# Recurrent network on one core: four PSUM banks each for gates and values in the attention, the spreading of 1/std in the layer norm, and another recurrent layer

## The chip, the cores and the metric

The kernel runs on one core of a Trainium2 chip. The metric is the time of one execution on the device in microseconds. All data is in float32. The engines are TensorE (PE, with its weight loads shown apart as PEld), VectorE (DVE), ScalarE (ACT), GpSimd (POOL) and SyncE (SP), which here only issues DMAs. Each engine works through its own instructions in order; semaphores hold it where it needs another's result.

## What is computed

The input x is an image of 256 by 256 positions with 32 channels. Four layers are added onto it, each on a group-normalised copy.

```python
x = x + L0(_gn(x))      # layer norm, value and gate products, sigmoid, output product
x = x + L1(_gn(x))      # 3x3 mean, two Sobel filters, magnitude
x = x + L2(_gn(x))      # the same once more
x = x + L3(_gn(x))      # recurrent: 256 sequences of 256 steps, two layers of 128 units

# L0: the softmax is summed over the axis that is contracted with it, so it adds up to 1:
o = sigmoid(mn @ Wg) * (mn @ Wv);   return o @ Wo + bo        # mn = layer norm over channels
# L3, one step; z = x_t @ W_lat + b_lat, then for both layers j:
zz = concat([z, h[j]]) @ W_cell[j] + b_cell[j]
zz = group_norm(zz, 4 groups) * gn_gamma[j] + gn_beta[j]
i, f, o, g = split(zz, 4)
c = sigmoid(f) * c + sigmoid(i) * tanh(g);   h = sigmoid(o) * tanh(c);   z = z + h
# x_hat = x_t + z @ W_out + b_out
```

In the inputs the recurrent norm's weights gn_gamma are 1 and gn_beta are 0.

## The kernel before

The image lies in SBUF as 64 blocks of four rows by 32 channels on the 128 partitions, with the 256 sequences (positions along the other axis) on the free axis: `xa`, and a second copy `xb`. Work on it goes two blocks (512 columns) at a time, 32 such pairs, counted by k.

**Layer norm (L193 to L240).** Per pair, a product with `cen` subtracts the mean over channels (`pc`), ACT squares it, DVE writes it to `xb`, and four products with one column per block give the variances (`pvar`). After eight pairs the 1/std of the batch is computed, transposed and kept in `rstdt`. The framework's scheduler sets the order here.

**Attention (L244 to L314).** `normed(k)` multiplies 1/std back onto the channels: four products with the constant `spread` (`pb`, L256), a product on DVE (L265), and weight and bias on POOL (L267). `gate(u)`, one half (128 of 256 channels) of a pair, does four gate products and four value products, each on 32 rows for one row of the block, all in a pool of six PSUM banks (`pgv`, L277); ACT takes the sigmoid (L283), DVE the product (L285). `project(u)` collects the output in `po` (L293), two units later. The order is written out by hand.

**Recurrence (L557 to L743).** The 256 sequences are two halves h of 128, and there are two layers l, so that one time step has four units (l, h), each with its own PSUM bank `zz` of 128 sequences by 512 gate values. A unit's chain is, by the names of the plan: x, the product with the input (33 rows, one of them the bias); i, the product with layer 0's new state (layer 1 only); m, the product with its own last state; sq, the squares on ACT; rd, their sums on DVE; pw, the power -1/2 on POOL; nz, the scaling on DVE; sg and tg, sigmoid and tanh on ACT; ig, fc and c, the new cell (DVE, POOL, DVE); th, its tanh on ACT; h, on DVE; T, the transpose on TensorE; e, its copy to SBUF on ACT, for the next m. Means are zero by construction, since weights and bias have been centred per gate.

The dictionary `PLAN` gives each operation a time within a step of `PERIOD`; all operations of all steps are sorted by it, and written out in that order. So the numbers set the order in every queue, and nothing else: on the chip each engine runs on as soon as its inputs are there.

In the version before, inputs and `fx` lie twice, at partitions 0 and 64; "x" of a unit issues two 33-row products, one for each layer, in different row groups. The output sums (`emit`) are done once in four steps, as products of 32 columns wide, eight of them. `recurrent_weights` tests on DVE whether the norm's weights are 1 and 0 (`off`, `least`, `flag`), and a branch takes one of two arms; with these inputs it is the one where nz is one multiplication.

## Time and profile before

| what | value |
|---|---|
| median of 3 runs | 3559.14 us (3511.32 to 3562.1) |
| the profiled execution's own time | 3559.14 us |
| its span (first to last instruction) | 3557.3 us |
| PE busy | 91% |
| DVE busy | 77% |
| ACT busy | 57% |
| POOL busy | 49% |

By stretch, from the trace's table of windows: the input and its transposes until 52 us; layer norm 52 to 163.5; attention and its group norm 163.5 to 487; the two Sobel layers 487 to 919; weights of the recurrence 919 to 955.5; the recurrence 955.5 to 3551; the last output until the end.

How to read it: a share is busy time over the span. A group's row names line, engine, operation, what it writes and reads with its shape, and how often; then the busy time in us, the mean duration of one in ns, and after a second bar the idle time ahead of it and what ended that. In timelines the first two numbers are start and length in us. A float32 product shows as two records (x2), each with its own weight load on PEld. The granted clock is TensorE's, as a share of the full one.

### The profile page before, as it was taken

The numbers are of one execution on the slowest core, as the hardware profiler recorded it, in microseconds if no ns is written. First come the engines' busy times: TensorE is split into PE (matmuls) and PEld (weight loads), VectorE is DVE, ScalarE is ACT, GpSimd is POOL, SyncE is SP. The second block draws the span as 40 slices with busy tenths as digits, with TensorE's granted clock in tenths as the row PEclk, the third lists the DMA queues.
The fourth block names the chain that finished last, engine by engine and source line by source line (L and its number), as shares of the span: only waits on it lengthen the run. The fifth ranks groups of instructions, "written<-read, shape, count | busy, mean of one in ns | idle before, by whom it ended". The sixth has DMA issues, their size and how long they took to land.

```text
span 3557.3 us, 40880 instructions
## 1 busy us (share of the span) xinstructions
PE 3245.7 (91%) x11221; PEld 1349.6 (38%) x11221; DVE 2728.8 (77%) x6064; ACT 2037.8 (57%) x5784; POOL 1747.8 (49%) x2358
## 2 busy tenths in 40 slices
PE   6999988798799999999999999999999999999998
PEld 4643356576333333333333333333333333333332
DVE  3267786686588888888888888888888888888886
ACT  3244443333366666666666666666666666666665
POOL 0000034454355555555555555555555555555554
PEclk7599999999799999999999999999999999999998
DMA  3000000000100000000000000000000000000000
GB/s 108 0 1 1 1 1 1 1 1 1 30 7 7 13 13 7 15 7 13 7 13 7 13 13 7 13 10 13 8 12 7 12 8 13 13 9 14 1 7 7
DMA packets 29944, 38.52 MB, mean 11 GB/s; under 512 B 6244, under 2 KB 22917, under 8 KB 29704
## 3 DMA queue, kind: packets, MB, share of 16 engines
q1 hardware_dynamic: 27392, 33.57, 3.3%
q10 hardware_dynamic: 2312, 2.25, 0.2%
q8 instruction: 90, 1.47, 0.2%
q14 instruction: 150, 1.23, 0.1%
HBM read 10.63 MB, written 8.39 MB: 5 GB/s over the span
## 4 chain that ended last, share of the span: by engine, by line
PE 76%; DVE 8%; ACT 7%; issue 3%; POOL 3%; DMA 0%; ACTq 0%; POOLq 0%; DVEq 0%
PE zz L628 26%; PE zz L612 15%; PE zz L623 15%; PE pgv L277 6%; ACT hT L691 4%; PE pt L687 3%; POOL ss L387 2%; PE px L701 2%; PE po L293 2%; PE pc L217 2%; DVE pp L348 1%; PE pvar L225 1%; DVE zn L648 1%; DVE dh L354 1%; PE pb L256 1%
## 5 line engine op out<-in xcount | busy, mean ns | idle before, releaser
L628 PE MATMUL zz<-wc,hT 128*128 128x512 f32 x2040 | 1083.3, 633 | 161.6 <-ACT hT L691 152.8
L644 POOL TENSOR_TENSOR rs<-ve,mhalf 128x4 f32<-128x4 f32 x1024 | 1053.5, 1029 | 208.4 <-DVE ve L641 208.0
L673 POOL TENSOR_TENSOR fc<-ga,c 128x128 f32<-128x128 f32 x1020 | 466.0, 457 | 881.1 <-ACT ga L664 870.9
L648 DVE TENSOR_TENSOR zn<-zz,rs 128x512 f32<-128x512 f32 x1024 | 700.8, 684 | 128.3 <-POOL rs L644 128.3
L641 DVE TENSOR_REDUCE ve<-sq 128x4 f32<-128x516 f32 x1024 | 699.8, 683 | 63.2 <-ACT sq L636 47.9
L636 ACT ACTIVATE sq<-zz 128x512 f32<-128x512 f32 x1024 | 605.9, 592 | 114.8 <-PE zz L628 109.6
L691 ACT COPY hT<-pt 128x128 f32<-128x128 f32 x1024 | 248.2, 268 | 655.1 <-PE pt L687 650.8
L612 PE MATMUL zz<-fx,xt 33*128 33x512 f32 x2048 | 585.7, 644 | 11.3 <-DVE zn L648 7.6
L623 PE MATMUL zz<-wc,hT 128*128 128x512 f32 x1024 | 578.1, 646 | 0.0
L664 ACT ACTIVATE ga<-zn 128x384 f32<-128x384 f32 x1024 | 535.8, 523 | 61.2 <-DVE zn L648 61.2
L628 PEld LDWEIGHTS zz<-wc,hT 128*128 128x128 f32 x2040 | 325.1, 189 | 528.9 <-ACT hT L691 408.8
L669 DVE TENSOR_TENSOR c<-ga 128x128 f32<-128x128 f32 x1024 | 331.9, 324 | 106.0 <-ACT ga L666 105.5
L684 DVE TENSOR_TENSOR h<-ga,th 128x128 f32<-128x128 f32 x1024 | 331.3, 324 | 70.7 <-ACT th L681 57.5
L677 DVE TENSOR_TENSOR c<-c,fc 128x128 f32<-128x128 f32 x1020 | 294.5, 289 | 82.2 <-DVE c L669 2.3
L681 ACT ACTIVATE th<-c 128x128 f32<-128x128 f32 x1024 | 313.5, 306 | 63.7 <-DVE c L677 63.6
L666 ACT ACTIVATE ga<-zn 128x128 f32<-128x128 f32 x1024 | 314.1, 307 | 0.0
L612 PEld LDWEIGHTS zz<-fx,xt 33*128 33x128 f32 x2048 | 156.2, 185 | 405.0 <-DVE c L677 334.5
L623 PEld LDWEIGHTS zz<-wc,hT 128*128 128x128 f32 x1024 | 152.6, 188 | 389.7 <-issue 388.9
L687 PEld LDWEIGHTS pt<-ident,h 128*128 128x128 f32 x1024 | 144.1, 141 | 350.9 <-DVE h L684 228.2
L687 PE MATMUL pt<-ident,h 128*128 128x128 f32 x1024 | 247.1, 281 | 13.3 <-DVE h L684 5.9
L267 POOL TENSOR_SCALAR mn<-mn,gamma,beta 128x512 f32<-128x512 f32 x32 | 24.7, 771 | 444.5 <-DVE mn L265 444.5
L283 ACT ACTIVATE sg<-pgv 128x512 f32<-128x512 f32 x256 | 139.1, 597 | 171.2 <-PE pgv L277 164.3
(130 smaller groups left out, 2720.6 us busy)
## 6 DMA issues: line engine op xcount, KB each, us to landing
xt<-xa SPq DMA_DIRECT2D x256, 64.0 KB, 2.0
nat<-in_x_dram SPq DMA_DIRECT2D x16, 512.0 KB, 6.4
out_dram<-st SPq DMA_DIRECT2D x32, 256.0 KB, 2.3
wc<-in_L_conv_W_cell_dram ACTq DMA_DIRECT2D x2, 512.0 KB, 4.1
kt<-in_consts_dram ACTq DMA_DIRECT2D x1, 832.0 KB
wv<-in_L_conv_Wv_dram ACTq DMA_DIRECT2D x4, 32.0 KB, 4.4
wg<-in_L_conv_Wg_dram ACTq DMA_DIRECT2D x4, 32.0 KB, 4.3
gamma<-in_L_conv_ln_gamma_dram ACTq DMA_DIRECT2D x4, 0.1 KB, 6.7
```

What stands on the lines that cost most here:

```text
L612: nc.tensor.matmul(zz, lhsT=x, rhs=fx[rows, l, :], start=True, stop=l == 0 and t == 0)
L623: nc.tensor.matmul(get("zz"), lhsT=v["hT", 0, t][:, seqs], rhs=wc[:, l, 0, :], start=False, stop=t == 0)
L628: nc.tensor.matmul(get("zz"), lhsT=v["hT", l, t - 1][:, seqs], rhs=wc[:, l, 1, :], start=False, stop=True,)
L636: nc.scalar.activation(sqs[l, h][:, :, 0:H], four(get("zz")), AF.Square, scale=float(H**-0.5))
L641: nc.vector.tensor_reduce(ve, sqs[l, h], AX.X, ALU.add)
L644: nc.gpsimd.tensor_tensor(rs, get("ve"), mhalf, ALU.pow)
L648: nc.vector.tensor_mul(four(zn), four(get("zz")), get("rs").unsqueeze(2).to_broadcast([P, 4, H]))
L664: nc.scalar.activation(ga[:, 0 : 3 * H], get("zn")[:, 0 : 3 * H], AF.Sigmoid)
L669: nc.vector.tensor_mul(c, gates(get("ga"), 0), gates(get("ga"), 3))
L673: nc.gpsimd.tensor_mul(fc, gates(get("ga"), 1), get("c"))
L687: nc.tensor.transpose(pt[:, 0:P], get("h"), ident)
L691: nc.scalar.copy(v["hT", l, t][:, seqs], get("pt")[:, 0:P])
```

## The change

**Norm and attention.** `rstdt` becomes a small tile per batch. The `pb` products, their product on DVE and the weights on POOL move from `normed` into the norm's loop, right behind the batch's transpose, in place on `xb`; `pc` and `pb` have two banks each. In the attention, gates and values get pools of four banks each, and the output `pg` of `project` takes one of the gates' banks. The order is gate, value, next gate, value, project for the pair before.

```diff
-        name="ps_ln", bufs=3, space=PSUM
+        name="ps_ln", bufs=2, space=PSUM
...
-            nc.scalar.copy(rstdt[:, bat, :], ptr)
+            rstdt = lnp.tile([P, P], F32, name="rstdt", bufs=2)
+            nc.scalar.copy(rstdt, ptr)
+            for i in range(KB):
+                k = bat * KB + i
+                pb = ps_ln.tile([P, 2, 2, P], F32, name="pb", bufs=2)
+                for b in range(2):
+                    for h in range(2):
+                        r = (i * 2 + b) * 2 + h
+                        nc.tensor.matmul(
+                            pb[:, b, h, :],
+                            lhsT=spread[:, r * J : (r + 1) * J, :].rearrange("p j c -> p (j c)"),
+                            rhs=rstdt,
...
+                nc.vector.tensor_mul(xc, xc, pb.rearrange("p b h s -> p (b h s)"))
+                nc.gpsimd.tensor_scalar(xc, xc, gamma4, beta4, ALU.mult, ALU.add)
...
-        name="ps_at", bufs=6, space=PSUM
-    ) as ps_at, tc.tile_pool(name="ps_o", bufs=1, space=PSUM) as ps_o:
+        name="ps_g", bufs=4, space=PSUM
+    ) as ps_g, tc.tile_pool(name="ps_v", bufs=4, space=PSUM) as ps_v:
...
+            gate(0)
+            for k in range(NST):
+                value(2 * k)
+                gate(2 * k + 1)
+                value(2 * k + 1)
+                if k >= 1:
+                    project(k - 1)
+                if k + 1 < NST:
+                    gate(2 * k + 2)
+            project(NST - 1)
```

**Recurrence.** The test, the branch and the second copy of inputs go. x is one product of all 128 rows, of which 95 are zero. The squares are four activations, one per gate, that sum as they go; `ve` on POOL adds the epsilon. nz is four operations that also multiply by gamma, and bz adds beta. One sigmoid covers all four gates; the tanh of g is 2 sigmoid(2g) - 1, with the factor 2 in gamma and beta, and ig is (s - 0.5) times the input gate, with th scaled by 2. For the output, hs adds the two layers' states on POOL, and one product per step with `woutz` (zero outside 32 columns) sums it. The plan's PERIOD is 10.34 instead of 8.78, with other times.

```diff
-        rows = slice(l * X1, l * X1 + KX)
-        x = xts[blk // XT % NX][rows, blk % XT, j, h * P : (h + 1) * P]
-        nc.tensor.matmul(zz, lhsT=x, rhs=fx[rows, l, :], start=True, stop=l == 0 and t == 0)
+            x = xts[blk // XT % NX][:, blk % XT, j, seqs]
+            nc.tensor.matmul(zz, lhsT=x, rhs=fx[:, l, :], start=True, stop=l == 0 and t == 0)
...
-            nc.scalar.activation(
-                sqs[l, h][:, :, 0:H], four(get("zz")), AF.Square, scale=float(H**-0.5)
-            )
-        elif name == "rd":
-            nc.vector.tensor_reduce(ve, sqs[l, h], AX.X, ALU.add)
+            for g in range(4):
+                nc.scalar.activation(
+                    sq, gates(get("zz"), g), AF.Square, accum_out=ss[:, g : g + 1]
+                )
+        elif name == "ve":
+            nc.gpsimd.tensor_scalar(ve, get("ss"), 1.0 / H, CELL_EPS, ALU.mult, ALU.add)
...
-                nc.vector.tensor_mul(
-                    four(zn), four(get("zz")), get("rs").unsqueeze(2).to_broadcast([P, 4, H])
-                )
+            for g in range(4):
+                nc.vector.scalar_tensor_tensor(
+                    gates(zn, g),
+                    gates(get("zz"), g),
+                    get("rs")[:, g : g + 1],
+                    gates(gam[:, l, :], g),
+                    ALU.mult,
+                    ALU.mult,
+                )
+        elif name == "bz":
+            nc.vector.tensor_add(get("zn"), get("zn"), bet[:, l, :])
...
-            nc.scalar.activation(ga[:, 0 : 3 * H], get("zn")[:, 0 : 3 * H], AF.Sigmoid)
-        elif name == "tg":
-            nc.scalar.activation(gates(get("ga"), 3), gates(get("zn"), 3), AF.Tanh)
+            nc.scalar.activation(ga, get("zn"), AF.Sigmoid)
...
+        elif name == "hs":
+            nc.gpsimd.tensor_add(v["hs", t][:, seqs], v["hT", 0, t][:, seqs], v["hT", 1, t][:, seqs])
...
+        nc.tensor.matmul(px, lhsT=woutz[:, j, :], rhs=v["hs", t], start=False, stop=j == J - 1)
...
-PERIOD = 8.78
+PERIOD = 10.34
 PLAN = {
+    (0, 0): dict(x=-2.2, m=0, sq=1.5, ve=2.8, pw=3.08, nz=4.16, bz=5.2, ga=5.95, fc=7.22, ig=7.6),
+    (0, 1): dict(x=2.96, m=5.17, sq=6.67, ve=7.97, pw=8.25, nz=9.33, bz=10.37, ga=11.12, fc=12.39),
+    (1, 0): dict(x=9.18, i=11.45, m=12.45, sq=13.72, ve=15.02, pw=15.3, nz=16.38, bz=17.34),
+    (1, 1): dict(x=14.35, i=16.62, m=17.62, sq=18.89, ve=20.19, pw=20.47, nz=21.55, bz=22.51),
 }
+PLAN[0, 0].update(c=7.9, th=8.35, h=8.71, T=9.07, e=9.71)
+PLAN[0, 1].update(ig=12.78, c=13.07, th=13.52, h=13.88, T=14.24, e=14.88)
+PLAN[1, 0].update(ga=18.17, ig=18.85, fc=19.57, c=20.51, th=20.87, h=21.32, T=21.68, e=21.98, hs=22.31)
+PLAN[1, 1].update(ga=23.34, ig=24.02, fc=24.74, c=25.68, th=26.04, h=26.49, T=26.85, e=27.15, hs=27.48)
```

## The prediction

> **What bounds the kernel now.** I read the table of busy time by stretch first, then the chain of waits and the timeline inside one time step, then the groups. The stretches (columns: stretch, length, then busy time and instructions of PE, PEld, DVE, ACT, POOL, then the granted clock, DMA share, GB/s):
>
> ```profile
> 52.00:163.50 111.50, 110.07 (x324) 76.54 (x324) 28.01 (x37) 23.93 (x39) 0.00 (x0) 0.50 0.00 0
> 163.50:487.00 323.50, 318.90 (x1793) 127.02 (x1793) 224.26 (x352) 141.96 (x259) 24.83 (x34) 0.97 0.00 1
> 955.50:3551.00 2595.50, 2416.90 (x7412) 832.88 (x7412) 2126.41 (x5180) 1686.42 (x5183) 1500.27 (x2047) 0.99 0.04 10
> ```
>
> These are the layer norm, the gated attention and the recurrence. The recurrence is 73% of the span: 2595.5/256 = 10.14 us a step, so 0.1 us a step is worth 25.6 us, more than most edits elsewhere. The chain of waits inside two steps says what holds it:
>
> ```profile
> by line: PE zz L628 34.6%; PE zz L612 25.2%; PE zz L623 23.1%; ACT hT L691 5.2%; PE pt L687 4.5%; DVE zn L648 2.8%; PE px L697 2.1%; DVE st L718 2.0%; issue 1.6%; PE pf L717 1.1%; DVE h L684 1.0%
> ```
>
> TensorE's three gate products are 83% of the chain. The timeline tells what one product costs (start, length, engine):
>
> ```profile
> 2002.40 1.98 PE L628 MATMUL zz<-wc,hT 128*128 128x512 f32 x4 [0.25 <-ACT hT L691]
> ...
> 2002.93 0.19 PEld L628 LDWEIGHTS zz<-wc,hT 128*128 128x128 f32 x1 [0.24 <-ACT ga L664]
> ...
> 2003.36 0.19 PEld L628 LDWEIGHTS zz<-wc,hT 128*128 128x128 f32 x1 [0.24 <-issue]
> ...
> 2004.31 0.30 PEld L612 LDWEIGHTS zz<-fx,xt 33*128 33x128 f32 x4 [0.76 <-DVE c L677]
> 2004.31 1.13 PE L612 MATMUL zz<-fx,xt 33*128 33x512 f32 x4
> ...
> 2005.37 0.30 PEld L623 LDWEIGHTS zz<-wc,hT 128*128 128x128 f32 x2 [0.76 <-issue]
> 2005.37 1.12 PE L623 MATMUL zz<-wc,hT 128*128 128x512 f32 x2
> ...
> 2008.82 1.13 PE L628 MATMUL zz<-wc,hT 128*128 128x512 f32 x2 [0.35 <-ACT hT L691]
> ```
>
> One product alone takes 1.13 us (2008.82), two of them together 1.98: the second adds 0.85, because its weights were loaded at 2002.93 while the first still ran. Around the 33-row x products nothing is loaded ahead: the loads at 2004.31 and 2005.37 start when the product before has ended, and each product fills 1.06 us. A step now has four m, two i and two pairs of x (a pair runs side by side in 1.06).
>
> **The recurrence, engine by engine.** TensorE: the x products become four full-height ones. Ten full-height products at 0.85 are 8.5 us, four transposes at 0.11 (chain) 0.45, and the output sums, now 1.25 products of 256 columns a step at 0.43 (L697 in the chain) plus transposes, 0.6. That is 9.6 us a step: more work than before, but it fits into 10.14, and the order puts an x product between each transpose and the m that needs it, where PE now stands still (0.35 us at 2008.82). So what is late next are the other engines.
>
> The Trainium skill speaks against my 0.85: "TensorE: Matmul & The Clock Gate", The mechanism, has weight loads overlap running matmuls only where the row groups differ. By that rule every product would cost 1.06 and TensorE alone 11.7 us a step. The row at 2002.93, both full height, shows the overlap, and the x rows show none where the row groups change; I go by the rows.
>
> The other engines per unit (four units a step), with the rows they come from:
>
> ```profile
> L644 POOL TENSOR_TENSOR rs<-ve,mhalf 128x4 f32<-128x4 f32 x1024 | 1053.5, 1029 | 208.4 <-DVE ve L641 208.0
> L648 DVE TENSOR_TENSOR zn<-zz,rs 128x512 f32<-128x512 f32 x1024 | 700.8, 684 | 128.3 <-POOL rs L644 128.3
> L636 ACT ACTIVATE sq<-zz 128x512 f32<-128x512 f32 x1024 | 605.9, 592 | 114.8 <-PE zz L628 109.6
> ```
>
> - sq: one 592 ns activation becomes four 128x128 ones that also sum. No row has a summing activation. Short activations start 0.20 us apart here (2009.77, 2009.97, 2010.17) and last 0.31 (L681); the ends are 0.20 and 0.31 and more. I take 0.29, near the upper end, since the sum must also be written; the new plan leaves 1.16 for four. First start to last end: 3x0.29+0.31 = 1.18.
> - the 683 ns reduction on DVE (L641) goes; ve, 128x4 on POOL, comes: 0.32 (L341; 0.22 to 0.60), with 0.05 of handing over 0.37.
> - pw stays at 1.03.
> - nz: one 684 ns product becomes four scalar_tensor_tensor of 128x128, 0.34 each (L535, a single one), started 0.26 apart if they overlap by the 0.08 that plain products show (0.28 long, 0.20 apart); ends 0.20 and 0.34. Then bz, an addition of 128x512, 0.68, that needs them and 0.1 for the dependence (L669 at 2005.17 for 0.28, L677 at 2005.56): 3x0.26+0.34+0.1 = 1.22 to its start.
> - sg and tg become one sigmoid of 512, 0.63 long (L664's 0.52 plus 0.11 for 128 more); ig becomes 0.34; hs adds 0.46 on POOL (L673's shape).
>
> All queues are in order, and the order is written out by hand. Walking round it, the longest loop in half a step goes from one layer's squares to the other half's: squares 1.18, ve 0.37, pw 1.03, hand-over 0.03, nz 1.22, bz until the next start 0.60, ig until c may start 0.44, c 0.32 with hand-over, th until the next sq may start 0.20. Sum **5.39 us**. A second loop (nz, the other half's c, bz, ga 0.53, e 0.20, sq) has 5.31. TensorE needs 4.8, and the pure dependence of layer 0 on itself 8.4 a step, so neither is the bound. On top: the output's fin (0.47 on ACT) and st (0.42 on DVE) every fourth step and px ahead of an m, 0.1 a half step; and one conflict:
>
> ```profile
> 492.27 0.71 DVE L348 TENSOR_TENSOR pp<-u,xn 128x508 f32<-128x508 f32 x1
> ...
> 494.27 1.42 POOL L352 TENSOR_TENSOR sh<-v 128x512 f32<-128x512 f32 x1
> 494.71 1.52 DVE L348 TENSOR_TENSOR pp<-u,xn 128x508 f32<-128x508 f32 x1
> ```
>
> The same DVE addition took 0.71 alone and 1.52 beside a POOL addition. The new bz is such an addition, and by the walk fc (0.46 on POOL) falls on its start: between 0 and 0.3 a half step; I take 0.07, the loops having some play. Half a step 5.56, a step **11.1 us**: (11.1-10.14)x256 = **+246 us**. The ends: squares 0.20, nz 0.20 apart and no conflict give 9.95 a step (-49 us); squares 0.35, nz 0.34 apart and the full conflict 12.3 (+553 us).
>
> **Norm and attention.** These lines are one unit of attention (9.77 us for two units and one pb):
>
> ```profile
> 196.12 1.14 PE L277 MATMUL pgv<-mn,wg 32*128 32x512 f32 x8
> 197.08 2.45 PE L277 MATMUL pgv<-mn,wv 32*128 32x512 f32 x8
> 198.20 2.48 DVE L285 TENSOR_TENSOR o<-pgv,sg 128x512 f32<-128x512 f32 x4 [2.22 <-PE pgv L277]
> 199.47 1.06 PE L293 MATMUL po<-o,wo 128*32 128x512 f32 x8
> ```
>
> The value products take 2.45 instead of 1.14 since with six banks they wait for sigmoids to free them. With four banks for each, PE needs 4x0.96 + 1.92 = 5.8 a pair and DVE 2x2.4 + 1.4 (L302, L303) = 6.2. The project's 1.9, the next gate's 0.96 and a first value's 1.1 stand in PE's order ahead of the next o: 0.1 to 0.2 (last value's end) + 4.1 against 3.8 of DVE work leaves some 0.5 idle: 6.8. Saved: (9.77-6.8)x32 = 95 us, and of the 11 us that the stretch holds beyond 32x9.77, for filling, I leave 6: 100. pb moves into the norm, which has PE full at clock 0.50: its 8 records took 2.0 to 2.1 us there (164 to 176 us) against 1.16 later: 32x2.0 = +64 if the clock stays. pb also makes that stretch denser, so some of it may run at the full clock: I take +40, so **-60**; ends -14 (+64, and 7.5 a pair) and -118 (the norm no longer than now with pb in it, at the full clock, and 6.3 a pair). DVE's product (0.69) and POOL's 0.77 lie beside PE there.
>
> The page's States table (same title, What's actually happening) has the clock rise after 3.4 us of sustained work; by that the norm, 99% busy, should be at full clock already and pb cost 37 us. The row says 0.50 for 111 us.
>
> **The start of the recurrence.** Now 11 us of memsets (L572) run after the weights are done at 943.7, behind the branch; the first reduction waits for them until 955.6. Without the branch they go ahead, beside the weights; the 3.6 us of flag tests on DVE go too. **-10** (0 to -13). x loads are halved to four per block; SP has room either way.
>
> Sum, against the profiled execution's 3559.1 us, which is also the median of the three: 3559+246-60-10 = **3735 us**.
>
> **Rivals.** A, *TensorE is relieved and nothing replaces it*: squares start 0.20 apart, scalar_tensor_tensor 0.20, step 9.95: 3559-49-70 = 3440, faster. For: the short activations at 2009.77 to 2010.17 start 0.20 apart, and an x product stands where PE now waits. Against: the sum's extra write, and DVE then holds 9 to 10 us. It decides from a step under 10.13, where the other parts' 70 us are the whole change. B, *the play swallows most of it*, step 10.13 to 10.69 (the plan writes 10.34): about 3556, no change. C, *conflict and serial small instructions*, step 11.9: 3559+451-70 = 3940. That the change doesn't do what it says would be an attention that only loses pb (8.7 a pair, 34+5-40, nothing saved): 3795.
>
> Chances: forecast (step 10.7 to 11.5) 0.50, A 0.10, B 0.17, C 0.23. Faster by over 2% (about what a measurement can tell here) 0.10, within 0.17, slower 0.73. Range 3500 (step 10.2) to 3900 (11.75), leaving out most of A and half of C.
>
> **What would show it.** Step by step: recurrence stretch/256 near 11.1; TensorE's share of its chain well under 83%, with DVE, ACT and POOL in its place; weight loads inside running matmuls throughout, x products adding 0.85; squares 0.29 apart; bz longer than 0.68 beside fc; attention 6.8 us a pair. A summing activation at 0.20 or at 0.4 makes the forecast wrong most easily: 0.1 on it is 0.3 on the half step, 150 us in all.

## The result and the profile after

The changed kernel takes **4072.67 us** (median of 4 runs, 4070.23 to 4088.86), the kernel before 3535.23 us on the same chip (4 runs, 3510.25 to 3562.1). The ratio is 1.153 (95% interval 1.141 to 1.165; the runs of the kernel before lie near 3510 or near 3560, which makes most of its width): slower, as forecast, but by far more; 3735 us was forecast and 3900 the end of the range. The profiled execution has a time of 4088.86 us and a span of 4086.5 us. It is the one that the sums below are made against.

The table of busy time by stretch of the changed kernel (stretch, length, busy time and instructions of PE, PEld, DVE, ACT, POOL, then clock, DMA share, GB/s) answers to the three lines shown of before: norm, attention, and recurrence.

```profile
52.00:162.00 110.00, 107.31 (x581) 83.39 (x580) 47.02 (x69) 24.20 (x40) 23.20 (x31) 0.81 0.00 1
162.00:410.00 248.00, 244.09 (x1536) 104.35 (x1536) 203.21 (x322) 130.20 (x257) 1.41 (x4) 1.00 0.00 1
880.50:4080.00 3199.50, 2667.87 (x6897) 1092.30 (x6897) 2529.03 (x8251) 2547.08 (x11320) 2286.09 (x3580) 1.00 0.02 6
```

The last statistics of the attention end at 409.6 us, where they ended at 487.2: 77.6 us won, 60 were forecast. The recurrence takes 3199.5/256 = **12.50 us a step** where 10.14 were and 11.1 were forecast: +604 us. What lies between, from the group norm's aggregate to the first step of the recurrence, is 38.5 us (842.0 to 880.5), where it was 36.8. The Sobel layers between take 0.8 more. 3557.3 - 77.6 + 0.8 + 1.7 + 604 = 4086.2, against a span of 4086.5: the change of time is in these places, and nearly all of the loss is in the recurrence.

The profile page's chain of work that ended last, by engine and by line, for the changed kernel:

```profile
POOL 50%; issue 19%; DVE 14%; PE 12%; ACT 4%; POOLq 0%; DMA 0%; ACTq 0%; DVEq 0%
POOL rs L616 23%; POOL ve L613 13%; POOL fc L643 8%; DVE zn L620 6%; POOL hs L665 4%; DVE zn L629 3%; PE pg L271 3%; POOL ss L389 2%; PE pv L271 2%; PE pg L296 1%; DVE pp L350 1%; ACT ga L632 1%; PE pc L216 1%; DVE dh L356 1%; ACT mag L391 1%
```

In the recurrence before, 83% of the chain were TensorE's gate products. Now TensorE has 12% of the whole chain, 7% of it in norm and attention (pg, pv, pc), and GpSimd's power, the small ve and fc have 44%. TensorE was relieved, as the prediction said. That POOL leads this chain doesn't make POOL the bound: it is busy for 2286 of the 3199.5 us, and stands idle ahead of ve until the squares on ACT end (681.8 us in the row of ve below). The chain goes back along POOL's own queue there and books that wait as "issue", so that the squares don't show in it. The loop that the prediction walked goes through them; it is walked again further down.

The costliest groups (line, engine, operation, tiles and shapes, count; busy us and mean ns of one; idle time before and what ended it):

```profile
L620 DVE SCALAR_TENSOR_TENSOR zn<-zz,rs,gam 128x128 f32<-128x128 f32 x4096 | 1152.9, 344 | 484.9 <-POOL rs L616 484.5
L608 ACT ACTIVATE sq<-zz 128x128 f32<-128x128 f32 x4096 | 1130.6, 276 | 100.7 <-PE zz L590 2.2
...
L613 POOL TENSOR_SCALAR ve<-ss 128x4 f32<-128x4 f32 x1024 | 560.3, 547 | 777.1 <-ACT sq L608 681.8
...
L608 ACT ACTIVATION_READ_ACCUMULATOR sq<-zz 128x1 f32 x4096 | 800.6, 195 | 0.0
```

Two rows differ from the sum of the prediction. A summing activation is two instructions, one of 276 ns and one of 195 ns that reads the sum out. And ve, four numbers per partition, takes 547 ns on average, where the sum had 0.32 us.

The timeline of one half step, and of one more ve further on (start, length, engine and line), shows both:

```profile
2004.42 0.26 ACT L608 ACTIVATE sq<-zz 128x128 f32<-128x128 f32 x1
...
2004.58 0.19 ACT L608 ACTIVATION_READ_ACCUMULATOR sq<-zz 128x1 f32 x1
...
2004.80 0.28 ACT L608 ACTIVATE sq<-zz 128x128 f32<-128x128 f32 x1
...
2005.77 0.19 ACT L608 ACTIVATION_READ_ACCUMULATOR sq<-zz 128x1 f32 x1
...
2006.00 0.69 DVE L629 TENSOR_TENSOR zn<-zn,bet 128x512 f32<-128x512 f32 x1
2006.05 0.89 POOL L613 TENSOR_SCALAR ve<-ss 128x4 f32<-128x4 f32 x1 [0.90 <-ACT sq L608]
...
2007.03 1.01 POOL L616 TENSOR_TENSOR rs<-ve,mhalf 128x4 f32<-128x4 f32 x1
...
2009.23 0.69 DVE L629 TENSOR_TENSOR zn<-zn,bet 128x512 f32<-128x512 f32 x1
...
2009.77 0.20 POOL L613 TENSOR_SCALAR ve<-ss 128x4 f32<-128x4 f32 x1 [0.61 <-ACT sq L608]
...
2018.70 0.69 DVE L629 TENSOR_TENSOR zn<-zn,bet 128x512 f32<-128x512 f32 x1
2018.75 0.69 POOL L613 TENSOR_SCALAR ve<-ss 128x4 f32<-128x4 f32 x1 [0.90 <-ACT sq L608]
```

The four squares start 0.40 us apart and hold ACT from 2004.42 to 2005.96. ve starts 0.05 after beta's addition (bz, L629, two inputs in SBUF, 128x512), and ends 0.25 after it: 0.89 us. The next ve starts when bz has only 0.15 us left and takes 0.20. The usual case is the one at 2018.75: ve starts 0.05 after bz and ends 0.05 after it, 0.69 us.

### The profile page after: what moved, and what is told of

The parts are those of the page before. It is cut to its first block, busy times and chain, and to the rows that moved or that the text cites. A ratio compares the mean times of both kernels' runs of the same rounds, so it can differ in the third digit from the quotient of the medians.

```text
span 4086.5 us, 52371 instructions
## 1 busy us (share of the span) xinstructions
PE 3420.8 (84%) x10709; PEld 1593.9 (39%) x10709; DVE 3131.6 (77%) x9136; ACT 2888.4 (71%) x11928; POOL 2534.0 (62%) x3891
## 4 chain that ended last, share of the span: by engine, by line
POOL 50%; issue 19%; DVE 14%; PE 12%; ACT 4%; POOLq 0%; DMA 0%; ACTq 0%; DVEq 0%
POOL rs L616 23%; POOL ve L613 13%; POOL fc L643 8%; DVE zn L620 6%; POOL hs L665 4%; DVE zn L629 3%; PE pg L271 3%; POOL ss L389 2%; PE pv L271 2%; PE pg L296 1%; DVE pp L350 1%; ACT ga L632 1%; PE pc L216 1%; DVE dh L356 1%; ACT mag L391 1%
## 5 line engine op out<-in xcount | busy, mean ns | idle before, releaser
L620 DVE SCALAR_TENSOR_TENSOR zn<-zz,rs,gam 128x128 f32<-128x128 f32 x4096 | 1152.9, 344 | 484.9 <-POOL rs L616 484.5
L608 ACT ACTIVATE sq<-zz 128x128 f32<-128x128 f32 x4096 | 1130.6, 276 | 100.7 <-PE zz L590 2.2
L590 PE MATMUL zz<-fx,xt 128*128 128x512 f32 x2048 | 1050.8, 595 | 3.4 <-issue 3.4
L613 POOL TENSOR_SCALAR ve<-ss 128x4 f32<-128x4 f32 x1024 | 560.3, 547 | 777.1 <-ACT sq L608 681.8
L632 ACT ACTIVATE ga<-zn 128x512 f32<-128x512 f32 x1024 | 644.2, 629 | 427.5 <-POOL ve L613 342.9
L608 ACT ACTIVATION_READ_ACCUMULATOR sq<-zz 128x1 f32 x4096 | 800.6, 195 | 0.0
L629 DVE TENSOR_TENSOR zn<-zn,bet 128x512 f32<-128x512 f32 x1024 | 705.7, 689 | 17.6
L590 PEld LDWEIGHTS zz<-fx,xt 128*128 128x128 f32 x2048 | 373.8, 205 | 221.3 <-issue 114.9
L637 DVE SCALAR_TENSOR_TENSOR c<-ga 128x128 f32<-128x128 f32 x1024 | 294.8, 288 | 73.3 <-ACT ga L632 73.1
L665 POOL TENSOR_TENSOR hs<-hT,hT 128x128 f32<-128x128 f32 x512 | 233.2, 456 | 68.6 <-ACT hT L661 60.1
```

The costliest lines, as they stand in the source:

```text
L590: nc.tensor.matmul(zz, lhsT=x, rhs=fx[:, l, :], start=True, stop=l == 0 and t == 0)
L608: nc.scalar.activation(sq, gates(get("zz"), g), AF.Square, accum_out=ss[:, g : g + 1])
L613: nc.gpsimd.tensor_scalar(ve, get("ss"), 1.0 / H, CELL_EPS, ALU.mult, ALU.add)
L620: nc.vector.scalar_tensor_tensor(gates(zn, g), gates(get("zz"), g), get("rs")[:, g : g + 1], gates(gam[:, l, :], g), ALU.mult, ALU.mult,)
L629: nc.vector.tensor_add(get("zn"), get("zn"), bet[:, l, :])
L632: nc.scalar.activation(ga, get("zn"), AF.Sigmoid)
```

## The experiments

A common measure for all of them: there are four powers (rs) in a step, so that n powers in the 1000 us from 1500 to 2500 us of a trace make a step of 4000/n us. It gives 4000/397 = 10.08 for before and 4000/322 = 12.42 for the changed kernel. The medians of the kernel before beside the runs were 3508.9 to 3561.4 us; single times are compared with the changed kernel's 4072.67 (or, profile against profile, 4088.86). Where two traces differ in the norm as well, the recurrences alone are compared, from the first power to the last: 3192.4 us in the changed kernel.

**Norm and attention alone** (`att_only`): the first part of the change, as the diff shows it, put into the kernel before; the recurrence stays.

```diff
-            nc.scalar.copy(rstdt[:, bat, :], ptr)
+            nc.scalar.copy(rstdt, ptr)
+            for i in range(KB):
+                ...
-        name="ps_at", bufs=6, space=PSUM
+        name="ps_g", bufs=4, space=PSUM
+    ) as ps_g, tc.tile_pool(name="ps_v", bufs=4, space=PSUM) as ps_v:
```

> The kernel before with the changed norm and attention alone; its recurrence stays. If the parts are independent: the trace of the changed kernel has these two stages end at 412 us instead of 487, so some 75 us less than before (about 2% faster, near 3480 us), and the recurrence at 10.14 us a step as before. Then the whole loss, and 75 us more, lies in the recurrence. If the new attention leaves something behind that slows the recurrence (the order or the banks), its stretch is over 10.3 us a step.

Measured: 3470.0 us (3468.68 to 3478.86), ratio 0.983 (0.972 to 0.994) to the kernel before. Profiled spans: 3477.0 against 3557.3, 80 less; the medians are 39.7 apart (3470.0 against 3509.67 for the kernel before beside it). A step is 4000/398 = 10.05. The first part is a gain by itself and the whole loss is the recurrence's; this version is the fastest of the study.

**Squares that don't sum** (`no_read`; the kernel leaves the variances out):

```diff
...
-                nc.scalar.activation(
-                    sq, gates(get("zz"), g), AF.Square, accum_out=ss[:, g : g + 1]
-                )
+                nc.scalar.activation(sq, gates(get("zz"), g), AF.Square)
...
-            nc.gpsimd.tensor_scalar(ve, get("ss"), 1.0 / H, CELL_EPS, ALU.mult, ALU.add)
+            nc.gpsimd.tensor_scalar(ve, get("sq")[:, 0:4], 1.0, 1.0, ALU.mult, ALU.add)
```

> The changed kernel with squares that are not summed: the four activations stay, their sums are left out (the power is taken of four values of the last square plus 1, so that what follows still waits for it). Theory of the loop: each sum shows in the trace as a record of 195 ns of its own on ACT, squares start 0.40 us apart; without it 0.20, the squares shrink from 1.54 to about 0.9 us, 0.3 to 0.65 us a half step, and the run is 150 to 330 us below the changed kernel. Rival, TensorE's ten full-height products set the step: no change, within 40 us. Rival, GpSimd's load sets the step: no change either.

Measured: 3858.57 us, 214 less (213 in the recurrence), inside the 150 to 330 expected; a step is 11.59. Its timeline has the four squares of a unit in one line:

```profile
2002.48 1.21 ACT L607 ACTIVATE sq<-zz 128x128 f32<-128x128 f32 x4
```

Without sums they take 1.21, 0.3 apart, where the prediction had 1.18 and the changed kernel has 1.54. The difference of 0.33 to 0.36 a half step is 170 to 185 us, most of what was won. The rest comes with a shift: ve is down to 214 ns in this run, and fc, 458 ns in the changed kernel, is up to 644, since it is fc that meets bz here (0.90 us for those that start beside it, 0.46 for those that don't meet it).

**No second SBUF input in bz** (`bz_one_input`) and its control (`bz_scratch`): in the first, bz is an instruction of the same length that reads one tile; in the second it stays the addition of two tiles, but writes a tile that nobody reads, so that the sigmoid doesn't wait for it in either.

```diff
-            nc.vector.tensor_add(get("zn"), get("zn"), bet[:, l, :])
+            scr = up.tile([P, nc.vector.BN_STATS_DIM], F32, name="scr")
+            nc.vector.bn_stats(scr, get("zn"))
```
```diff
-            nc.vector.tensor_add(get("zn"), get("zn"), bet[:, l, :])
+            scr = up.tile([P, 4 * H], F32, name="scr")
+            nc.vector.tensor_add(scr, get("zn"), bet[:, l, :])
```

> The changed kernel with bz replaced by a statistics instruction of the same length (0.69 us) on the same tile, in the same place of DVE's queue, that reads one tensor from SBUF instead of two; the addition of beta is left out, and the sigmoid no longer waits for it. Theory that ve on GpSimd is held while DVE reads two tensors: ve falls from a mean of 0.55 to about 0.2 to 0.25 us, and the run is 130 to 200 us below the changed kernel. Theory that ve is slow for its own sake, or waits for something else: ve stays near 0.55, and the run is within 50 us of the changed kernel.

> The control to bz_one_input: bz stays an addition of two tensors in SBUF, in its place of DVE's queue, but writes to a tile that nobody reads, so that, as there, the sigmoid no longer waits for it (beta, which is 0, is left out). The two differ in the number of tensors read. Theory that two tensors hold GpSimd: ve has a mean near 0.5 us again, and the run is 100 us or more above bz_one_input (3875 us), at 3980 to 4080. Rival, the gain there came from the sigmoid that no longer waited: within 40 us of 3875, with ve near 0.2.

Measured: 3875.05 us with one input, 4048.39 with two. The groups of ve in the 1000 us, first with one input:

```profile
L613 POOL TENSOR_SCALAR ve<-ss 128x4 f32<-128x4 f32 x345 | 68.0, 197 | 200.1 <-ACT sq L608 173.6 <-DVE scr L630 13.4 <-DVE c L638 12.2
```

and with two:

```profile
L613 POOL TENSOR_SCALAR ve<-ss 128x4 f32<-128x4 f32 x324 | 162.5, 501 | 238.2 <-ACT sq L608 211.7 <-DVE scr L630 24.5 <-DVE zn L620 2.0
```

The pair differs in the second input, and in how much is written (6 columns instead of 512). Writing is not what holds POOL: fc runs beside nz, which writes 512 columns but reads one tile from SBUF and one from PSUM, in 944 of 1020 cases of the changed kernel, and takes 457 ns there. So it is the second input: ve 197 against 501 ns, and 173 us in all. The recurrences themselves are 190 us apart (2978.3 and 3167.9), 0.37 a half step; the times are closer because the norm ran at a granted clock of 1.00 from 60 us in the trace with two inputs, and at 0.50 until 90 us in the one with one, where the attention ends 15.5 us later. So the conflict is real and costs about 190 us; the sigmoid's wait for bz, gone in both, is worth only 24 us (4072.67 - 4048.39, and 24.5 in the recurrence).

**Less work on TensorE** (`no_x1`, which leaves layer 1's input product out), the rival that TensorE still sets the pace:

```diff
-            nc.tensor.matmul(zz, lhsT=x, rhs=fx[:, l, :], start=True, stop=l == 0 and t == 0)
+            if l == 0:
+                nc.tensor.matmul(zz, lhsT=x, rhs=fx[:, l, :], start=True, stop=t == 0)
...
```

> The changed kernel without layer 1's input product: two of the ten full-height products of a step are left out, 1.7 us of TensorE a step. Theory of the loop over ACT, POOL and DVE: TensorE has room, so within 60 us of the changed kernel. Rival, TensorE's extra work sets the step: 1.7 x 256 = 435 us less, or at least 200.

Measured: 4106.98 us, no gain from two products less a step (1.7 us of TensorE's time). The granted clock in its recurrence was 0.93 instead of 1.00, so that the other products took longer (671 ns instead of 605 a record for m), but TensorE's busy time still fell from 838 to 768 of 1000 us, and the time did not. The rival falls.

**Reduction instead of sums** (`sq_reduce`): one activation for the four squares, as in the kernel before, and the reduction on DVE in ve's place in the plan; nz and bz as changed.

```diff
...
-            for g in range(4):
-                nc.scalar.activation(
-                    sq, gates(get("zz"), g), AF.Square, accum_out=ss[:, g : g + 1]
-                )
+            nc.scalar.activation(
+                sqs[l, h][:, :, 0:H], four(get("zz")), AF.Square, scale=float(H**-0.5)
+            )
...
-            nc.gpsimd.tensor_scalar(ve, get("ss"), 1.0 / H, CELL_EPS, ALU.mult, ALU.add)
+            nc.vector.tensor_reduce(ve, sqs[l, h], AX.X, ALU.add)
```

> The changed kernel with the squares and their sums as before: one activation of 512 and a reduction on DVE in the place of ve; all else as changed. Theory of the loop: 1.54 + 1.07 at most for squares and ve become 0.62 + 0.82, so up to 1.2 us less a half step; but DVE then holds two reductions of 0.60 more a half step, 4.6 + 1.2 = 5.8 us, and becomes the bound: 5.8 to 6.0 a half step instead of 6.25, 130 to 230 us below the changed kernel. Rival, the squares are the whole loss: back to near 10.5 us a step, 500 us below.

Measured: 4979.55 us, a step of 16.0: a gain was expected and 900 us were lost. The chain over two steps:

```profile
by line: POOL rs L620 38.3%; DVE zn L624 26.8%; DVE ve L617 13.5%; DVE zn L633 10.2%; issue 7.2%; DVE c L651 3.3%; DVE c L641 3.1%; POOLq L620 0.4%; DVEq L651 0.3%
```

Power, nz, reduction and bz stand one behind the other. The theory had only durations in it. But the reduction, put on DVE, stands in DVE's queue behind an nz of the other layer, and that nz waits for its power: two trips through the power in each half step instead of overlapped ones.

**One multiplication for nz, no bz** (`nz_one`), with the former sigmoid and tanh; squares and ve as changed. The norm's weights are left out.

```diff
-            for g in range(4):
-                nc.vector.scalar_tensor_tensor(
-                    gates(zn, g), gates(get("zz"), g), get("rs")[:, g : g + 1], ...
+            nc.vector.tensor_mul(
+                four(zn), four(get("zz")), get("rs").unsqueeze(2).to_broadcast([P, 4, H])
+            )
...
```

> The changed kernel with the scaling and the gates as before: one multiplication for nz, no bz, sigmoid of three gates and a tanh (gamma of 1 and beta of 0 are left out); the summing squares and ve stay. Theory of the loop: nz 1.16 and bz 0.61 become 0.60, ve falls to 0.2 since no two-tensor addition of 512 is left: 1.54 + 0.38 + 1.05 + 0.60 + 0.38 + 0.33 + 0.22 = 4.5 a half step; ACT holds 5.2 with its sums and becomes the bound: 10.4 to 10.9 us a step, 400 to 540 us below the changed kernel. Rival, TensorE's full-height products are the loss: still over 11.5 us a step.

Measured: 3788.21 us, 284 less, a step of 11.30; less was won than expected. ACT is 86% busy and the summing squares have 33% of the chain: with DVE freed, they are the next bound.

**All operations as before, in the new order** (`all_ops`): the edits of the two last kernels together.

> The changed kernel with squares, sums, scaling and gates all as before (no test of the weights, gamma of 1 and beta of 0 left out), so that of the recurrence's change the full-height x products, the output sums of every step and the plan's order stay. Theory of the loop: it shrinks to 4.0 us a half step and TensorE with 4.8 sets the step: 9.6 to 10.3 us, 3340 to 3510 us in all, about 1 to 6% below the kernel before and at or below att_only (3470). Rival, the order or TensorE's extra work is the loss: over 11 us a step, over 3690 us.

Measured: 4082.55 us (4081.92 to 4100.19), ratio 1.162 (1.151 to 1.173). The same as the changed kernel, without any of its new unit operations but the x product, the output sums with hs, and the order: 570 us above the 3340 to 3510 expected, the second large miss of a theory that had only durations in it. DVE and POOL in its timeline:

```profile
2003.06 0.68 DVE L617 TENSOR_REDUCE ve<-sq 128x4 f32<-128x516 f32 x1
...
2003.89 1.13 POOL L620 TENSOR_TENSOR rs<-ve,mhalf 128x4 f32<-128x4 f32 x1 [1.07 <-DVE ve L617]
...
2005.05 0.69 DVE L624 TENSOR_TENSOR zn<-zz,rs 128x512 f32<-128x512 f32 x1 [0.91 <-POOL rs L620]
2005.66 0.68 DVE L617 TENSOR_REDUCE ve<-sq 128x4 f32<-128x516 f32 x1
...
2006.48 1.01 POOL L620 TENSOR_TENSOR rs<-ve,mhalf 128x4 f32<-128x4 f32 x1 [1.04 <-DVE ve L617]
...
2007.52 0.69 DVE L624 TENSOR_TENSOR zn<-zz,rs 128x512 f32<-128x512 f32 x1 [0.26 <-POOL rs L620]
```

The second reduction (2005.66) starts as soon as the nz before it (2005.05) has left DVE, which waited 0.91 us for the first power. Nothing else separates them: the order in the queue does.

**The reductions ahead of the other layer's nz** (`all_ops_order`): two numbers of the plan.

```diff
-    (1, 0): dict(x=9.18, i=11.45, m=12.45, sq=13.72, ve=15.02, pw=15.3, nz=16.38, bz=17.34),
-    (1, 1): dict(x=14.35, i=16.62, m=17.62, sq=18.89, ve=20.19, pw=20.47, nz=21.55, bz=22.51),
+    (1, 0): dict(x=9.18, i=11.45, m=12.45, sq=13.72, ve=14.45, pw=15.3, nz=16.38, bz=17.34),
+    (1, 1): dict(x=14.35, i=16.62, m=17.62, sq=18.89, ve=19.62, pw=20.47, nz=21.55, bz=22.51),
```

> The kernel with the former unit operations in the new order (one activation for the squares, the reduction on DVE, one multiplication, sigmoid and tanh), and two numbers of the plan changed: layer 1's reductions go 0.57 earlier, so that each stands in DVE's queue ahead of the other layer's nz instead of behind it. Like its parent it leaves the norm's weights (1 and 0) out. Order theory: the parent's 6.13 us a half step are two trips through the power one behind the other, because the second reduction waits behind an nz that waits for the first power; with the reductions ahead of it the two powers follow each other on POOL, and half a step falls to 4.9 to 5.3, where TensorE (4.8) is the next bound: 3380 to 3600 us. If the order in DVE's queue isn't the cause, it stays within 80 us of 4083.

Measured: 3780.77 us (3778.98 to 3795.57), ratio 1.070 (1.058 to 1.082). 302 us less by two numbers, with no operation changed: the order theory holds, though a step is 11.30 and not the 9.8 to 10.6 expected. A stretch of its chain (start, length, what):

```profile
2000.44 0.29 DVE c L645
...
2000.82 0.32 ACT th L649
2001.14 0.02 issue
2001.16 0.30 DVE h L652
...
2001.51 0.34 PE pt L655
2001.85 0.02 issue
2001.87 0.28 ACT hT L659
2002.15 0.07 issue
2002.22 0.46 POOL hs L663
2002.67 0.43 POOL fc L641
2003.10 0.02 issue
2003.12 0.29 DVE c L645
```

One cell waits for the other half's transpose, because hs, the new addition for the output, stands ahead of fc on POOL: 2.68 us of the 5.65 of a half step.

**hs behind the next power**, in that kernel (`all_ops_hs`) and in the changed kernel as it is (`after_hs`):

```diff
-... e=21.98, hs=22.31)
+... e=21.98, hs=23.81)
-... e=27.15, hs=27.48)
+... e=27.15, hs=28.98)
```

> The kernel with the former unit operations and layer 1's reductions moved ahead, and two more numbers of the plan changed: hs, the addition for the output on POOL, stands 1.5 later, behind the next power instead of ahead of the other unit's fc. The norm's weights (1 and 0) are still left out. Theory of the edge through hs (cell, tanh, h, transpose, copy, hs, fc, cell: 2.7 of the 5.7 us of half a step): the cell no longer waits for the other half's transpose; half a step falls to 4.9 to 5.3, 3390 to 3590 us. If hs only filled time that another edge sets as well: 3700 to 3790.

> The changed kernel, nothing left out, with hs 1.5 later in the plan as in the other run. hs is 6.5% and fc 9.4% of its chain over two steps, but its main stations are the power, ve and the squares: I expect 0 to 0.35 us a half step, 3900 to 4080 us. If the edge through hs is a bound of its own of some 5.6 us a half step, below the 6.25 of the loop through the squares, nothing is won: 4050 to 4110.

Measured: 3637.62 us (3628.9 to 3645.76), ratio 1.024 (1.014 to 1.034), a step of 10.70: 143 us less, but 48 us above the expected range. In the chain of this kernel over two steps TensorE is back:

```profile
by line: PE zz L603 22.4%; PE zz L598 15.9%; PE zz L596 12.7%; issue 9.3%; PE pt L655 5.8%; DVE zn L624 5.0%; ACT sq L612 4.5%; ACT th L649 3.5%; POOL rs L620 3.4%; DVE h L652 3.4%; DVE c L645 3.3%; PE px L671 3.2%; DVE ve L617 2.5%; POOL h
```

In the changed kernel the same move gives 4063.26 us, 9 less than its median and inside both expected ranges, which shows no clear gain. It fits an edge through hs that lies there below the loop through squares, ve and nz.

**Both mis-sized terms out** (`both`): the edits of the squares that don't sum and of bz with one input together.

> The changed kernel with both disputed terms taken out at once: the squares don't sum (the epsilon step reads four columns of the squares instead, so the power is that of other numbers), and beta's addition is a one-input instruction that writes a scratch tile, so that beta is left out and the sigmoid waits for nz alone. If the loop of the prediction is right and only its squares and its conflict were mis-sized, half a step is about 5.1 to 5.3 us now (5.39 less 4x0.09 for squares 0.20 apart, plus 0.1 for the output): 10.2 to 10.6 a step and 3500 to 3610 us in all. If the two removals overlap (each of the two alone has moved the loop to another edge that the other removal does not shorten), it stays within 100 us of the better of the two alone, 3750 to 3860.

Measured: 3743.97 us, a step of 4000/360 = 11.11. That is the forecast's 3735 and 11.1, and not the 3500 to 3610 expected here. The expectation had priced squares without sums at 0.20 apart; they are 0.3 apart, which is what the forecast had for squares with sums. So this kernel has the forecast's sizes: 1.19 or 1.21 for squares, 0.21 for ve (0.37 with its hand-overs, as forecast), no conflict. Both terms together are 345 us, profile against profile (4088.86 - 3743.97). Its chain over two steps does not go through the squares, though:

```profile
by line: DVE zn L617 20.8%; POOL rs L613 12.0%; DVE scr L627 9.7%; issue 8.8%; DVE h L652 6.8%; PE zz L590 6.4%; PE zz L597 6.4%; PE pt L655 4.8%; DVE c L645 4.4%; POOL ve L610 3.3%; PE zz L592 3.2%; ACT th L649 3.1%; DVE c L635 2.1%; ACT f
```

DVE is 89% busy in it. It also lets the sigmoid start without bz. So the agreement is one of sizes; that the loop named in the prediction sets this kernel is not shown.

**ve away from the conflict**, in two ways. In the first (`one_pow`) the power reads the sums and gamma takes the factor; in the second (`ve_act`) ACT computes ve right behind the squares.

```diff
...
-            nc.gpsimd.tensor_scalar(ve, get("ss"), 1.0 / H, CELL_EPS, ALU.mult, ALU.add)
+            return
...
-            nc.gpsimd.tensor_tensor(rs, get("ve"), mhalf, ALU.pow)
+            nc.gpsimd.tensor_tensor(rs, get("ss"), mhalf, ALU.pow)
```
```diff
...
-            nc.gpsimd.tensor_scalar(ve, get("ss"), 1.0 / H, CELL_EPS, ALU.mult, ALU.add)
+            nc.scalar.activation(ve, ss, AF.Identity, scale=1.0 / H, bias=epst)
```

> The changed kernel without ve: the power reads the sums themselves, and gamma is scaled by the root of 128 instead; the epsilon of 1e-5 is left out. Beta's addition stays. If ve with its hand-overs is on the loop with the 1.07 us a half step that the trace of the changed kernel shows, and the power isn't stretched in its place, half a step falls from 6.25 by 0.7 to 1.0: 3560 to 3720 us. If what conflicts is whatever stands on POOL when beta's addition runs, the power takes the hit (1.03 becomes 1.4 or more), only 0.2 to 0.4 is won, and the time is 3870 to 3990.

> The changed kernel with ve on ACT, straight behind the squares; nothing is left out. Conflict theory as in the kernel without ve, but ACT holds about 0.45 us more a unit (0.25 for one short activation and a wait of about 0.2 for its own sums), which is on the loop: 0.25 to 0.55 won a half step, 3800 to 3960 us. If the power then takes the conflict: 3980 to 4100, no gain.

Measured: 3999.62 and 4095.56 us. In the first the power takes the hit, as the second theory had it, though the time is 10 us above that theory's range (its timeline):

```profile
2006.24 1.77 POOL L616 TENSOR_TENSOR rs<-ss,mhalf 128x4 f32<-128x4 f32 x1 [0.82 <-POOL fc L643]
...
2006.26 0.69 DVE L629 TENSOR_TENSOR zn<-zn,bet 128x512 f32<-128x512 f32 x1
```

1.77 us beside bz instead of 1.02; the mean of the power rises from 1046 to 1241 ns and fc's from 458 to 521. Taking the victim away moves the conflict to the next instruction on POOL. In the second kernel the power has 1168 ns, and ACT has a fifth activation of 297 ns behind the four squares: the squares have 29% of the chain, ga 11%. How its lack of a gain divides between the two was not separated.

## Why the prediction was wrong in size

**Right: TensorE is relieved, and TensorE's own price.** The x products take 0.86 in the chain of the changed kernel (L590), where 0.85 was forecast; TensorE has 12% of its chain. Leaving 1.7 us of its work out wins nothing. That the change would be slower was forecast for the right kind of reason, then: another loop than TensorE's.

**Right: the loop, in its members.** The walk from layer 1's squares of one half to those of the other in the timeline (2004.42 to 2010.77) has the same stations: squares 1.54 (1.18 forecast), ve with its hand-overs 1.07 (0.37), power 1.04 (1.06), nz until bz 1.16 (1.22), bz until ig 0.61 (0.60), until c 0.38 (0.44), until th 0.33 (0.32), until the next squares 0.22 (0.20). Six of eight terms are within 0.06; the sum is 6.35 instead of 5.39. This is a half step with a long ve. Averaged over 159 such walks between 1500 and 2500 us the terms are 1.55, 0.84, 1.10, 1.16, 0.61, 0.42, 0.33 and 0.22, in sum 6.22, a step of 12.44. Squares and ve with its hand-overs are 0.37 and 0.47 over the forecast, the other six together 0.01 under it.

**Wrong: squares at 0.29 apart.** The step drew it from short activations 0.20 apart and 0.31 long, with an allowance for the sum. The read-out is an instruction of its own of 195 ns in ACT's queue, and the distance is 0.40, outside the bounds of 0.20 and 0.35 that the step gave. The closing sentence of the prediction priced this case (0.4, some 150 us in all), but it got no chance of its own and no place in the range. Cost: 0.37 x 512 = 190 us; the experiment without sums, 213 with a shift elsewhere.

**Wrong: the conflict at 0.07, on bz and fc.** The step took it as a slowing of the DVE addition by fc on POOL, and trusted the loops' play to swallow most of it. bz stayed at 0.69 us. The victim is ve: it is released by the end of the squares, just when bz has begun, and ends after it. The loop goes through layer 1's ve alone, 0.67 us on average (0.42 for layer 0's); with its hand-overs it takes 0.84 where the sum had 0.37. That is 0.47 x 512 = 241 us on this station, and 190 net by the pair of experiments, since other waits of the loop grow when ve shrinks.

The trace of the kernel before had this conflict at its full size, in the very row from which the prediction took its 0.32 for ve (L341, "0.22 to 0.60"):

```profile
493.51 0.68 DVE L350 TENSOR_TENSOR v<-pp 128x514 f32<-128x514 f32 x1
493.67 0.60 POOL L341 TENSOR_SCALAR pp<-u 128x4 f32<-128x4 f32 x1 [1.18 <-DVE u L337]
```

L350 adds a tile to itself shifted by one, so it has two inputs in SBUF. All 16 of the 64 that took 0.49 us or more started during such an addition; the other 48 took 0.22 to 0.23, six of them beside a statistics instruction with one input. The spread was read as a range of prices, where it was two cases.

With the means of the walk, the two terms are 0.84 a half step over the sum of 5.39. The forecast had 0.17 on top of that sum, for the output and the conflict; neither is a station of the measured walk. 6.22 - 5.56 = 0.66 a half step is 338 us of the (12.50-11.1) x 256 = 358 that the recurrence took over the forecast; the remaining 20 are the difference between the step in the middle, 12.44, and the whole stretch over 256, and rounding. With 12 us at its start and in the Sobel layers, and -17 in norm and attention, from the paragraphs below, 3735 becomes 4088, against the profiled execution's 4088.86.

**The ends of the range.** Added up from the prediction's own terms, with 0.1 a half step for the output, its ends are 10.1 and 12.4 us a step rather than 9.95 and 12.3. The measured step lies at the worse one. The range was nevertheless drawn to 11.75 only.

**The smaller terms.** Attention takes 7.66 us a pair (9.77 before, 6.8 forecast). DVE's timeline of one pair:

```profile
199.61 0.75 DVE L304 SCALAR_TENSOR_TENSOR xa<-pg,bo,xa 128x512 f32<-128x512 f32 x1 [0.71 <-PE pg L296]
200.40 0.69 DVE L305 BATCH_NORM_STATS2 stats<-xa 128x6 f32<-128x512 f32 x1
201.69 4.87 DVE L290 TENSOR_TENSOR o<-pv,sg 128x512 f32<-128x512 f32 x8 [0.60 <-PE pv L271]
207.27 0.75 DVE L304 SCALAR_TENSOR_TENSOR xa<-pg,bo,xa 128x512 f32<-128x512 f32 x1 [0.71 <-PE pg L296]
```

DVE idles twice a pair, 0.71 until the project's products end and 0.60 until the first value; the prediction had 0.5 in all and 6.2 of work, DVE has 6.3. So the attention wins 76 us and not 100. The norm made up for it: it ends at 162, with the first gate product at 162.8, where it ended at 163.5 without `pb` in it. +40 was forecast and -1.5 came, which is the good end that the step had given (no longer than now, with `pb` in it). From the first `pb` products on (89.8 us) the clock rises, as the table by stretch shows; the last line is the same norm in another trace (`after_hs`), ahead of its first `pb`:

```profile
80.00:90.00 10.00, 10.00 (x29) 6.79 (x30) 3.20 (x4) 2.25 (x5) 0.00 (x0) 0.50 0.00 0
90.00:100.00 10.00, 10.00 (x77) 9.04 (x76) 4.70 (x8) 2.06 (x3) 3.08 (x4) 0.96 0.00 1
...
60.00:70.00 10.00, 10.00 (x61) 7.37 (x59) 4.05 (x6) 4.05 (x6) 0.00 (x0) 1.00 0.01 2
```

By the Trainium skill ("TensorE: Matmul & The Clock Gate", What's actually happening, the States table) 3.4 us of sustained work suffice for the full clock; here PE was busy for all of the 10 us with 0.50 granted, and got 0.96 when the mix of products had changed. But the changed mix is not needed: of the 15 traces with this norm, eight have 0.50 from 60 to 90 us, and seven have 1.00 from 60 us on, with the same products. Attention ends some 15 us earlier in the seven. What decides between the two is open. Both traces that were compared for the norm's term, before and after, began it at 0.50; no trace shows the kernel before with its norm at 1.00.

The start of the recurrence was to win 10 us and lost 2. The memsets did move beside the weights, but a new wait, which the prediction overlooked, took more than that won (timeline of the start):

```profile
851.45 6.18 DVE L435 TENSOR_SCALAR wc<-wc,wm 128x128 f32<-128x128 f32 x16
...
859.12 0.48 DVE L461 TENSOR_SCALAR gb<-gb 1x256 f32<-1x256 f32 x2
859.49 7.16 PE L478 MATMUL pb<-gb,ones 1*128 1x512 f32 x8 [11.89 <-DVE gb L461]
```

The doubling of gamma and beta for the tanh (L461) stands in DVE's queue behind all centring of weights, and the products that spread them (L478) wait for it: 17.5 us after the aggregate instead of 6.1 before. And 16 centrings took 6.18 us beside POOL's memsets (843.9 to 855.1), 3.21 before without them.

**What stays open.** The forecast's loop held only as long as its terms were long enough. With the former operations back the new order is still slower than the old one (1.024 times the kernel before after four numbers of the plan were moved, against 0.983 with the old recurrence and the same attention). TensorE has over half of that kernel's chain; what of the difference is its full-height x products and what the remaining order was not tried apart. The new unit operations in the old order were not run either.

## What to carry to other kernels

Where every queue is in order and the order is written out by hand, an operation's price is its duration plus what its place in the queue makes wait: walk round the loop with each queue's order in it, since two numbers of a plan were worth 302 us here, and a cheaper instruction in the wrong queue lost 900. A term without a row in the trace that sits on the loop of every step deserves a range as wide as its step count makes it, and the stated range should reach the worse end that the working gives. Where a row's durations spread (0.22 to 0.60), find out what ran beside the long ones before a price is taken from between. And a conflict between two engines is not swallowed by play when the loop brings the two together in every turn: here it came in 852 of 1024 units, and when the victim was taken away the next instruction became it.

## What was not expected of the hardware

An activation that also sums along its row is followed by a second instruction of 195 ns, and 128x128 ones then follow each other at 0.40 us, where 0.30 was measured without sums.

GpSimd on 128x4 numbers, beside a DVE addition of two SBUF tiles, did not slow down in proportion. Of 1024 ve in the changed kernel 852 started during the addition of beta. None ended before the addition did, and 750 ended 0.05 us after it, wherever in it they had started: 0.68 us long from 0.05 after its start, 0.50 from 0.24, 0.20 when it was nearly over. The other 102 ended up to 0.26 after it, for a reason that no run shows. The 164 that met no such addition took 0.195 on average, and a one-input instruction of the same length on DVE left ve at 197 ns. The Trainium skill ("SBUF — State Buffer", SBUF: two separate sides) tells of a port pair that one of the two holds for a whole instruction when the DVE operation has two SBUF inputs, while the other is blocked; the runs agree, and it decides the size: what is lost is the rest of the DVE addition, not a share of it.

TensorE's granted clock stood at 0.50 from 60 to 90 us with PE busy throughout in eight traces, and at 1.00 in seven others, for the same products. Where it was 1.00, the attention ended some 15 us earlier.
